# Two graph layers on one core: transposing the norms with VectorE and DRAM in place of TensorE

## Chip, core and metric

The kernel runs on one core of a Trainium2 chip. The metric is the device time of one execution in microseconds (us). The kernel before takes 2699.25 us, the median of three runs (2699.2 to 2702.12).

Names in the profile: PE is TensorE (its matrix products), PEld its weight loads, DVE is VectorE, ACT is ScalarE, POOL is GpSimd, SP is SyncE, which issues the transfers. All data is float32.

## What is computed

There are 64 graphs of 256 nodes with 512 features each (x is 64 x 256 x 512), and one adjacency matrix of 256 x 256 for all. Two layers follow each other, each with a norm ahead of it and x added after it. Cut to what matters:

```python
# layer 0
h = relu(layernorm(x))
hw = h @ W                                   # 512 -> 256
e = leaky_relu(hw @ a[0] + (hw @ a[1]).T, 0.2) + NEG * (1 - adj)
x = x + concat(softmax(e) @ hw, hw)
# layer 1: attention with 8 heads of 64
h = relu(layernorm(x))
q, k, v = (split_heads(h @ W.T + b) for W, b in ((Wq, bq), (Wk, bk), (Wv, bv)))
s = where(adj == 0, -inf, q @ k.T / 8)
x = x + (softmax(s) @ v) @ Wo.T + bo
```

## The kernel before

The graphs are taken two at a time: 32 groups of GB = 2 graphs (batches b), each batch of NT = 2 tiles of 128 nodes, so a group has GT = 4 tiles of 128 x 512. Of three groups in flight, one is in its attention, the next in its projections, the third in the first layer. Products with TensorE contract over the partitions, so the normed x (nodes on the partitions) has to be turned until the features lie on the partitions. This is done four times 128 x 128 for each tile:

```python
def norm_T(src, mv, name):
    ...                                          # ve = variance + EPS, on VectorE
    nc.gpsimd.tensor_tensor(rstd, ve, rexp, op=ALU.pow)     # 1 / sqrt, on GpSimd
    def normed(t):                               # on VectorE
        xn[t] = (src[t] - mean) * rstd           # (shortened; line 354)
    def put(t, dst):
        if t + 1 < GT:
            normed(t + 1)
        pt = mm(...)                             # a bank of PSUM
        for c in range(HP):                      # HP = 4
            transpose(pt[:, c, :], xn[t][:, c * P : (c + 1) * P], ident)   # TensorE
        nc.scalar.activation(dst, pt, AF.Relu)   # line 365
```

The projections and the last product are not made as eight block products but as seven, by the scheme of Strassen and Winograd. That scheme needs four sums of the operand's quadrants. GpSimd makes them, for the normed x (`sums`, 4 x 128x512 a group) and for the weighed values (`o_sums`, 4 x 128x256 a batch):

```python
def operand_sums(quads, sums):                   # lines 376 to 379
    a11, a12, a21, a22 = quads
    nc.gpsimd.tensor_add(sums[:, 0], a21, a22)
    nc.gpsimd.tensor_sub(sums[:, 1], sums[:, 0], a11)
    nc.gpsimd.tensor_sub(sums[:, 2], a11, a21)
    nc.gpsimd.tensor_sub(sums[:, 3], a12, sums[:, 1])
```

Attention goes by quads of four heads. `scores` makes sc on TensorE, exp on ScalarE, the product with the mask on VectorE and a first sum on GpSimd; `weigh`, one step later, makes the weighed values and their denominators:

```python
def scores(g, b, quad):
    for i in range(QH // 2):                     # two pairs of heads
        ...                                      # sc: two banks of PSUM
        for j in range(2):
            nc.scalar.activation(pair[:, j], sc[j], AF.Exp, scale=scale)         # line 572
        nc.vector.tensor_mul(pair, pair, maskT...)                               # line 573
        nc.gpsimd.tensor_add(ps[...], pair[:, :, 0, :], pair[:, :, 1, :])        # line 574

def weigh(g, b, quad, p, ps):
    ...                                          # pr: v times p; total: ones times ps
    nc.vector.reciprocal(r, total)               # line 604
    nc.vector.tensor_mul(oT[:, 2 * quad : 2 * quad + 2, :], pr, r...)            # line 605
```

`outputs` makes the last product py in seven parts, and VectorE adds each to x in place. The parts 1, 6, 5 and 3 accumulate in one bank of PSUM (`first`), the parts 2, 7 and 4 in another bank (7 and 4 share one). So each part has to wait until VectorE has read the one before it in the same bank:

```python
def outputs(g, b):
    sums = ...; operand_sums(halves(oT, P), sums)
    product(first, 1, True);   add(0, 0, first);  yield    # add: x += bank, line 628
    product(second, 2, True);  add(0, 0, second); yield
    product(first, 6, False);  add(1, 0, first);  yield
    product(second, 7, True);  add(1, 1, second); yield    # another bank
    product(first, 5, False);  add(1, 1, first);  yield
    product(second, 4, False); add(1, 0, second); yield
    product(first, 3, False);  add(0, 1, first)
    ...                                                    # out <- x
```

The main loop weaves these by strings. A group has four steps, one for each quad of each batch. u is one part of a projection (7 each of q, k and v), o one part of the last product, s one piece of the first layer (with the second norm at its end):

```python
steps = ("uosuoosuosoosuos", "uusususususu", "uosoosuosoosuos", "uusususususu")
for g in range(NG):
    projected = project(g + 1)
    short = first_layer(g + 2)
    for step, parts in enumerate(steps):
        weigh(*waiting)                          # of the step before
        if waiting[2] == NQ - 1: late = outputs(*waiting[:2])
        waiting = (g, b, quad, *scores(g, b, quad))
        if step == 1: load(g + 3)
        ...                                      # the string
```

Beside this the kernel judges whether its inputs allow exp without subtracting a maximum: `judge` bounds norms of the weights (products gram and square on TensorE). Its pieces lie in free places of the first groups. If it says no, a second version of the whole computation runs; for these inputs it does not. Most engines' order is left to a scheduler; only TensorE's is pinned to the order in the text.

Of the kernel before, what the change touches and what calls it, by code (L numbers as in the profile page):

```python
# [23 lines left out]
LARGEST_VALUE = 1e6  # L24

# [17 lines left out]
def bounded(  # L43
# [23 lines left out]
    nc = tc.nc  # L67
    B, N, D = x.shape
# [17 lines left out]
    psum = ctx.enter_context(tc.tile_pool(name="psum", bufs=1, space=bass.MemoryType.PSUM))  # L86

# [15 lines left out]


# [13 lines left out]
    xg = x.rearrange("(g b) (t p) d -> g p (b t) d", b=GB, p=P)  # L118
    og = out.rearrange("(g b) (t p) d -> g p (b t) d", b=GB, p=P)
# [3 lines left out]
    def load(g):  # L123
        xs[g] = big.tile([P, GT, D], F32, tag="x", name=f"x{g}", bufs=4)
        nc.sync.dma_start(xs[g], xg[g])

    load(0)


# [14 lines left out]
    for c in range(HP):  # L144
        for s in range(2):
            nc.vector.scalar_tensor_tensor(
                prod, w0_sb[:, c, 2:], 1.0, a_b[:, s, :], op0=ALU.mult, op1=ALU.mult,
                accum_out=w0_sb[:, c, s : s + 1],
            )
    edge = att.tile([P, NT, N], F32, tag="e", name="edge")  # L150
    nc.vector.tensor_scalar(edge, adj_i, 0.0, None, op0=ALU.not_equal)
# [6 lines left out]
    nc.vector.tensor_copy(maskT, pt)  # L158

    nc.vector.reduce_max(bad[:, 0, :], edge, axis=AX.X)  # L160
    nc.vector.tensor_scalar(bad[:, 0, :], bad[:, 0, :], 0.0, None, op0=ALU.is_equal)
    nc.vector.tensor_tensor(edge, edge, adj_i, op=ALU.not_equal)
    nc.vector.reduce_max(bad[:, 1, :], edge, axis=AX.X)

    load(1)
    load(2)


# [27 lines left out]
    rexp = const.tile([P, GT], F32, name="rexp")  # L196
    nc.gpsimd.memset(rexp, -0.5)
    ones = const.tile([P, P], F32, name="ones")
    nc.gpsimd.memset(ones, 1.0)

    def weight_sums(name):
        w = w_sb[name]
        first = nc.vector.tensor_sub(w[:, :, T3, :], w[:, :, W22, :], w[:, :, W12, :])
        after(first, latest[0])
        nc.vector.tensor_sub(w[:, :, T1, :], w[:, :, W12, :], w[:, :, W11, :])
        nc.vector.tensor_sub(w[:, :, T2, :], w[:, :, W22, :], w[:, :, T1, :])
        nc.vector.tensor_sub(w[:, :, T4, :], w[:, :, W21, :], w[:, :, T2, :])

    def last_bias():


        pb = mm("pb")
        for q in range(NQ):
            for half in range(2):
                b = small.tile([P, P], F32, tag="power", name=f"bv_{q}_{half}", bufs=1)
                nc.vector.tensor_scalar(b, ones, bv_col[:, half, q : q + 1], None, op0=ALU.mult)
                matmul(
                    pb, b, w_sb["o"][:, half, 2 * q : 2 * q + 2, :],
                    start=(q == 0 and half == 0), stop=(q == NQ - 1 and half == 1),
                )  # L220
        nc.vector.tensor_add(b_out, pb, b_out)


    def judge():
# [5 lines left out]
        nc.vector.memset(part, 0.0)  # L230
        junk = att.tile([P, D], F32, tag="junk", name="junk", bufs=1)

        def squares(col, *srcs):
            sums = small.tile([P, HP], F32, tag="sums", name=f"sums{col}", bufs=2)
            for i, src in enumerate(srcs):
                nc.scalar.activation(
                    junk[:, : src.free_size()], src, AF.Square, accum_out=sums[:, i : i + 1]
                )
            nc.vector.reduce_sum(part[:, col : col + 1], sums[:, : len(srcs)], axis=AX.X)

        for s in range(2):
            squares(s, w0_sb[:, :, s])
        squares(2, *[w0_sb[:, c, 2:] for c in range(HP)])
        wv = att.tile([P, HP, D // HP], F32, tag="block", name="wv_block", bufs=1)
        sums = small.tile([P, HP], F32, tag="sums", name="sums3", bufs=2)
        for c in range(HP):
            nc.sync.dma_start(
                wv, wvT[:, c * P : (c + 1) * P].rearrange("(c p) o -> p c o", p=P)
            )
            nc.scalar.activation(  # L250
                junk, wv.rearrange("p c o -> p (c o)"), AF.Square, accum_out=sums[:, c : c + 1]
            )
        nc.vector.reduce_sum(part[:, 3:4], sums, axis=AX.X)
        squares(4, bcol["q"])
        squares(5, bcol["k"])
        squares(6, bv_col.rearrange("p h q -> p (h q)"))
        nc.vector.reduce_max(part[:, 7:8], bad.rearrange("p a t -> p (a t)"), axis=AX.X)
        yield
        heads = const.tile([P, P], F32, name="heads")
        nc.vector.memset(heads, 0.0)  # L260
        for j in range(2):
            nc.vector.memset(heads[j * DH : (j + 1) * DH, j * DH : (j + 1) * DH], 1.0)
        rowsq = const.tile([P, 2, HP], F32, name="rowsq")
        for n, (name, src) in enumerate((("q", wqT), ("k", wkT))):
            for hp in range(HP):
                w = att.tile([P, HP, P], F32, tag="block", name=f"w{name}_block{hp}", bufs=1)
                nc.sync.dma_start(
                    w, src[:, hp * P : (hp + 1) * P].rearrange("(c p) o -> p c o", p=P)
                )
                yield  # L270
                gram = mm(f"gram_{name}{hp}")[:, :P]
                for c in range(HP):
                    matmul(
                        gram, w[:, c, :], w[:, c, :], start=(c == 0), stop=(c == HP - 1)
# [799 lines left out]
```

## Time and profile before

| what | value |
|---|---|
| time, median of 3 | 2699.25 us |
| span of the profiled run | 2697.3 us |
| granted TensorE clock | 0.993 |
| TensorE busy | 2620.4 us, 97% |
| VectorE busy | 1669.7 us, 62% |
| GpSimd busy | 1230.0 us, 46% |
| ScalarE busy | 835.9 us, 31% |
| moved by transfers | 78.49 MB, mean 29 GB/s |
| pt, the transposes of the norms | 1024 of 128x128 on TensorE |
| o_sums on GpSimd | 256 of 128x256, 727 to 1660 ns each in the mean of their line |
| mask multiply p on VectorE | 256 of 128x1024, mean 1588 ns |

A group of the profile is a line of the kernel with an engine, its operation, its result and operands, their shapes, the count, the busy time and the mean length of one. Idle time ahead of it is put down to the work whose end released it. In the timeline the first number is the start in us from the start of the span, the second the length of the merged instructions. Durations of TensorE overlap, as its instructions are pipelined; what one costs is therefore read from start to start.

### The profile page before, as it was taken

How to read it: one execution, taken by the hardware profiler on the slowest of the kernel's cores; microseconds unless marked ns; L12 is line 12 of the kernel's file. 1: busy time of each engine (PE TensorE's matmuls, PEld its weight loads, DVE VectorE, ACT ScalarE, POOL GpSimd, SP SyncE). 2: the span in 40 equal slices, each digit the busy share in tenths (PEclk: the TensorE clock that was granted, in tenths of full speed). 3: DMA queues.
4: the chain of work that ended last, by engine and by line, in shares of the span. 5: the costliest groups of instructions: out<-in, count | busy, mean ns of one | idle time of the engine just before them, and what ended most of it. 6: DMA issues, size and time to landing. Idle time of an engine off the chain costs nothing.

```text
span 2697.3 us, 41512 instructions
## 1 busy us (share of the span) xinstructions
PE 2620.4 (97%) x17150; PEld 2118.8 (79%) x17150; DVE 1669.7 (62%) x2558; ACT 835.9 (31%) x1771; POOL 1230.0 (46%) x1004
## 2 busy tenths in 40 slices
PE   5999999999999999999999999999999999999997
PEld 3888888878888887887788888788878878878874
DVE  5666566666557665566665576665576656666544
ACT  2333232333332333323333323333333333233321
POOL 2353355443445443545434454435455335445343
PEclk8999999999999999999999999999999999999998
DMA  5000101000001010000000000000000000000000
GB/s 164 1 12 32 36 24 36 13 32 32 28 32 36 9 36 32 24 32 9 32 32 24 32 32 9 32 32 24 32 32 9 32 32 24 32 17 23 17 16 25
DMA packets 45890, 78.49 MB, mean 29 GB/s; under 512 B 3712, under 2 KB 10624, under 8 KB 45696
## 3 DMA queue, kind: packets, MB, share of 16 engines
q1 hardware_dynamic: 45696, 75.77, 8.1%
q8 instruction: 137, 2.24, 0.3%
q14 instruction: 57, 0.47, 0.1%
HBM read 42.21 MB, written 33.55 MB: 28 GB/s over the span
## 4 chain that ended last, share of the span: by engine, by line
PE 89%; DVE 8%; POOL 1%; issue 1%; DMA 0%; ACT 0%; DVEq 0%
PE pq L113 15%; PE pv L113 14%; PE py L113 13%; PE pk L113 13%; PE pr L113 9%; PE ph L113 8%; PE sc L113 7%; PE po L113 4%; PE pt L116 4%; DVE p L573 3%; DVE r L604 2%; PE total L113 2%; DVE k L544 1%; DVE oT L605 1%; PE pn L116 1%
## 5 line engine op out<-in xcount | busy, mean ns | idle before, releaser
L573 DVE TENSOR_TENSOR p<-p,maskT 128x1024 f32<-128x1024 f32 x256 | 398.6, 1588 | 0.6 <-ACT p L572 0.5
L572 ACT ACTIVATE p<-sc 128x512 f32<-128x512 f32 x512 | 264.4, 602 | 380.9 <-PE sc L113 380.9
L574 POOL TENSOR_TENSOR ps<-p 128x512 f32<-128x512 f32 x256 | 366.2, 1447 | 0.0
L628 DVE TENSOR_TENSOR x<-py,x 128x256 f32<-128x256 f32 x448 | 187.6, 419 | 272.8 <-PE py L113 266.9
L604 DVE RECIPROCAL r<-total 128x256 f32<-128x256 f32 x128 | 224.5, 1754 | 194.6 <-PE total L113 194.6
L113 PE MATMUL py<-wo_sb,o_sums 128*128 128x256 f32 x1024 | 266.5, 384 | 26.4 <-DVE x L628 21.6
L420 POOL TENSOR_TENSOR x<-H,x 128x256 f32<-128x256 f32 x128 | 87.7, 685 | 443.0 <-ACT H L419 441.9
L113 PE MATMUL pr<-p,v 128*32 128x256 f32 x4096 | 251.8, 385 | 5.8 <-DVE p L573 5.8
L113 PE MATMUL sc<-q,k 64*128 64x256 f32 x2048 | 255.7, 389 | 0.0
L113 PE MATMUL pq<-sums,wq_sb 128*128 128x256 f32 x1024 | 246.7, 384 | 4.2 <-POOL sums L377 3.7
L113 PE MATMUL ph<-w_sb,hT 128*128 128x258 f32 x1024 | 246.1, 383 | 0.0
L113 PE MATMUL pk<-sums,wk_sb 128*128 128x256 f32 x1024 | 244.8, 382 | 0.0
L113 PE MATMUL pv<-wv_sb,sums 128*128 128x256 f32 x1024 | 242.0, 379 | 0.1
L113 PEld LDWEIGHTS sc<-q,k 64*128 64x128 f32 x2048 | 187.2, 186 | 69.7 <-issue 52.6
L113 PEld LDWEIGHTS py<-wo_sb,o_sums 128*128 128x128 f32 x1024 | 191.2, 192 | 62.9 <-POOL o_sums L377 37.6
L365 ACT ACTIVATE hT<-pt 128x512 f32<-128x512 f32 x256 | 153.1, 599 | 266.0 <-PE pt L116 265.7
L354 DVE TENSOR_SCALAR xn<-x,mv,rstd 128x512 f32<-128x512 f32 x256 | 225.8, 893 | 9.5 <-PE pt L116 4.9
L376 POOL TENSOR_TENSOR o_sums<-oT 128x256 f32<-128x256 f32 x64 | 106.2, 1660 | 262.6 <-DVE oT L605 262.6
L113 PEld LDWEIGHTS pq<-sums,wq_sb 128*128 128x128 f32 x1024 | 190.1, 191 | 39.1 <-issue 9.9
L113 PEld LDWEIGHTS ph<-w_sb,hT 128*128 128x128 f32 x1024 | 195.7, 192 | 28.6
L113 PEld LDWEIGHTS pk<-sums,wk_sb 128*128 128x128 f32 x1024 | 189.3, 190 | 33.9 <-issue 9.9
L113 PEld LDWEIGHTS pr<-p,v 128*32 128x32 f32 x4096 | 121.1, 110 | 112.2 <-issue 39.7
(145 smaller groups left out, 4054.4 us busy)
## 6 DMA issues: line engine op xcount, KB each, us to landing
x<-in_x_dram SPq DMA_DIRECT2D x32, 1024.0 KB, 5.5
out_dram<-x SPq DMA_DIRECT2D x64, 512.0 KB, 2.8
wq_sb<-in_L_gnn_Wq_dram SPq DMA_DIRECT2D x2, 512.0 KB, 11.7
wk_sb<-in_L_gnn_Wk_dram SPq DMA_DIRECT2D x2, 512.0 KB, 12.4
wv_sb<-in_L_gnn_Wv_dram SPq DMA_DIRECT2D x2, 512.0 KB, 11.4
wo_sb<-in_L_gnn_Wo_dram SPq DMA_DIRECT2D x8, 128.0 KB, 3.3
wv_block<-in_L_gnn_Wv_dram SPq DMA_DIRECT2D x4, 256.0 KB, 3.0
wq_block<-in_L_gnn_Wq_dram SPq DMA_DIRECT2D x4, 256.0 KB, 2.9
```

The source lines that it names most:

```text
L113: in_order(nc.tensor.matmul(*args, **kwargs))
L116: in_order(nc.tensor.transpose(*args))
L354: latest[0] = nc.vector.tensor_scalar(xn[t], src[:, t, :], mv[:, t, 0:1], rstd[:, t : t + 1], op0=ALU.subtract, op1=ALU.mult,).ins.name
L365: nc.scalar.activation(dst, pt, AF.Relu)
L376: nc.gpsimd.tensor_add(sums[:, 0], a21, a22)
L420: nc.gpsimd.tensor_add(xt[:, t, F1:], H[:, t, 2 : F1 + 2], xt[:, t, F1:])
L544: nc.vector.tensor_add(part(1, 1), first, p7)
L572: nc.scalar.activation(pair[:, j], sc[j], AF.Exp, scale=scale)
L573: nc.vector.tensor_mul(pair, pair, maskT[:, None, :, :].to_broadcast([P, 2, NT, N]))
L574: nc.gpsimd.tensor_add(ps[:, 2 * i : 2 * i + 2, :], pair[:, :, 0, :], pair[:, :, 1, :])
L604: nc.vector.reciprocal(r, total)
L628: nc.vector.tensor_add(to, out, to)
```

## The change

The norms' tiles are no longer turned by TensorE. VectorE turns each block of 32 by 32 in place (one instruction for a tile of 128 x 512), a transfer writes a batch's two tiles to DRAM (512 KB), and four transfers bring them back with the blocks at their places, 1 KB at a time. ScalarE then applies the relu from SBUF in place of PSUM. Group 0 still uses TensorE, as it has nothing to hide the transfers behind. The aim is to take the transposes off TensorE.

Further, VectorE makes the quadrant sums of the weighed values in place of GpSimd, right after the weighed values in its order. `not_sooner` pins an instruction behind the one of its engine that stands ahead of it in the text. The norm is made for each batch and not for each tile. The judge moves ahead of the main loop and takes its weights from what is loaded already. x is loaded by batch (7 buffers), and the bias of the last product is added to x one group later. The strings of the steps are as before, but the pieces of the first layer are cut anew, and some of them are empty to give the transfers time.

The diff, cut to its core:

```diff
+    def not_sooner(engine, operation, *args, **kwargs):
+
+        last = engine.last
+        after(getattr(engine, operation)(*args, **kwargs), last)
...
     def stats(mv, src, t, name):
...
+        if vector.last:
+            not_sooner(vector, "bn_stats", st, src[t])
...
+        def norm(b):
...
+            gpsimd.tensor_tensor(rstd, ve, rexp, op=ALU.pow)
+            for t in range(NT):
+                r = b * NT + t
+                xn[r] = att.tile([P, D], F32, tag="xn", name=f"xn{name}_{r}", bufs=2)
+                not_sooner(
+                    vector, "tensor_scalar", xn[r], src[r], mv[:, r, 0:1], rstd[:, t : t + 1],
+                    op0=ALU.subtract, op1=ALU.mult,
+                )
...
+            for t in tiles:
+                not_sooner(
+                    vector, "transpose",
+                    xt[:, :, :, t % NT, :], xn[t].rearrange("p (c j a) -> p j c a", j=J, a=S),
+                )
+                turned[t] = moved[:, :, :, t % NT, :].rearrange("p i c n -> p c i n")
+            nc.sync.dma_start(passed, xt.rearrange("p j c t n -> p j (c t n)"))
+            for j in range(J):
+                nc.sync.dma_start(
+                    moved[j * S : (j + 1) * S].rearrange("a i c t n -> a i (c t n)"),
+                    passed.rearrange("(i a) j e -> j a i e", a=S)[j],
+                )
...
+                    not_sooner(scalar, "activation", to, turned[b * NT + t], AF.Relu)
...
+    def operand_sums(engine, quads, sums):
         a11, a12, a21, a22 = quads
-        nc.gpsimd.tensor_add(sums[:, 0], a21, a22)
...
+        not_sooner(engine, "tensor_add", sums[:, 0], a21, a22)
+        engine.tensor_sub(sums[:, 1], sums[:, 0], a11)
...
     def first_layer(g):
...
+        norm(0)
         yield GAP
...
+        turn(0)
+        norm(1)
+        yield GAP
+        turn(1)
+        yield GAP
+        yield GAP
+        put(0, hT[0])
+        yield GAP
+        for r in range(GT):
...
+            if r == NT - 1:
+                put(1, hT[1])
...
+            if r == 2:
+                norm(0)
+            elif r == 3:
+                turn(0)
...
+        norm(1)
         yield GAP
...
+        turn(1)
+        yield GAP
+        put(0, hT[:, :, :N])
+        yield GAP
+        put(1, hT[:, :, N:])
...
+        operand_sums(gpsimd, quads, sums)
...
     def weigh(g, b, quad, p, ps):
...
         if quad == NQ - 1:
             places.append(v_tag)
...
+            operand_sums(vector, quads, sums)
...
+            if step == 1 and g + 1 < NG:
+                residual(g + 1)
+            if step % 2 and g + 3 < NG:
+                load(g + 3, b)
```

## The prediction

> **What bounds the kernel now.** I read the table of busy shares first, then the slices, then the waits of TensorE, and last the timeline of one group in the middle of the run. From the page:
>
> ```profile
> PE 2620.4 (97%) x17150; PEld 2118.8 (79%) x17150; DVE 1669.7 (62%) x2558; ACT 835.9 (31%) x1771; POOL 1230.0 (46%) x1004
> PE   5999999999999999999999999999999999999997
> ```
>
> TensorE works in every slice but the first and the last at 9 tenths or more; its waits by releaser sum to few microseconds (the largest, py on x of L628, is 21.6 us of 2697). So a microsecond of matrix work taken away is a microsecond won, unless another engine then makes TensorE wait. What the transposes cost is read from the timeline of TensorE by start times, since the durations there overlap:
>
> ```profile
> 1001.68 0.60 PE L116 MATMUL pt<-ident,xn 128*128 128x128 f32 x4
> 1002.11 1.89 PE L113 MATMUL pv<-wv_sb,sums 128*128 128x256 f32 x8
> 1003.84 0.60 PE L116 MATMUL pt<-ident,xn 128*128 128x128 f32 x4
> ```
>
> A burst of four transposes (one 128x512 tile) takes 1002.11 - 1001.68 = 0.43 us, one product of the projections 1.73 us. There are 8 bursts a group (2 norms, 4 tiles), 256 in the run.
>
> 62% for VectorE is a mean. One group is four steps (a step is weigh, scores, and what its string of u, o and s adds). I cut the group at the starts of pr and asked for the busy time by engine in the four stretches:
>
> ```profile
> 1010.43:1031.09 20.66, 20.66 (x140) 17.00 (x139) 10.79 (x15) 6.75 (x14) 12.10 (x10) 1.00 0.00 1
> 1031.09:1053.70 22.61, 22.61 (x145) 18.53 (x144) 7.68 (x9) 8.01 (x19) 7.10 (x6) 1.00 0.20 71
> 1053.70:1073.90 20.20, 19.58 (x127) 15.64 (x126) 16.00 (x30) 5.03 (x11) 6.41 (x5) 1.00 0.00 1
> 1073.90:1092.39 18.49, 18.49 (x132) 15.01 (x131) 16.93 (x27) 6.39 (x13) 12.69 (x10) 1.00 0.08 30
> ```
>
> The columns are length, then PE, weight loads, DVE, ACT, POOL busy. TensorE fills all four; VectorE is busy 16.0 of 20.2 us in step 2 and 16.9 of 18.5 in step 3, but only 10.8 and 7.7 in steps 0 and 1.
>
> [...] no transpose is in this trace, but bn_stats over the same 512 elements is 691 ns (median), so I take 0.65 us from start to start for one tile: an estimate from that row. [...] the mask multiply (L573) takes 1212 ns at least, 1742 at the median, 2291 at most. [...]
>
> ```profile
> 1012.87 1.76 DVE L604 RECIPROCAL r<-total 128x256 f32<-128x256 f32 x1 [3.35 <-PE total L113]
> 1014.66 0.69 DVE L605 TENSOR_TENSOR oT<-pr,r 128x512 f32<-128x512 f32 x1
> 1015.26 3.23 DVE L573 TENSOR_TENSOR p<-p,maskT 128x1024 f32<-128x1024 f32 x2
> 1018.42 0.41 DVE L628 TENSOR_TENSOR x<-py,x 128x256 f32<-128x256 f32 x1
> ```
>
> Two multiplies take 3.23 us in place of 2.4, beside GpSimd's o_sums. The reader is also to see the chain: from the reciprocal at 1012.87 to the first x at 1018.42, all in VectorE's own order. The third product py, at 1020.16, writes the bank that this x has to have read first.
>
> **Part 1, removed from TensorE.** Groups 1 to 31 lose 8 bursts each: 248 x 0.43 = 107 us. TensorE's work by step then is: step 0, 20.66 less 3 bursts (1.30), one ph that moves to step 1 (1.75) and a square of the judge (0.22) = 17.4; step 1, 22.61 + 1.75 - 0.43 = 23.9; step 2, 20.20 less a wait (0.62) and a square (0.22) = 19.4; step 3, 18.49 - 4 x 0.43 - 0.22 = 16.5. Sum 77.2 in place of 81.96: without any new wait -4.7 us a group, over some 30 groups -140 us, 2560 us.
>
> **Part 2, added to VectorE.** 248 transposes x 0.65 = 161 us, and 64 x 4 sums of 128x256 at some 0.35 us from start to start (x of L628, same size, is 0.42 long) = 90 us. 1670 + 251 = 1921 us still is below 2560. But where it stands counts. In the built program's order of VectorE, all of the first norm now lies in step 0, pinned behind what precedes it: 4 bn_stats, 4 xn, 4 transposes, and 3 of the o_sums. In the kernel before, the bn_stats of that norm run in the last step of the group ahead. That makes 10.79 + 2.7 (bn_stats) + 0.7 (aggr) + 1.1 (two more xn) + 2.6 (transposes) + 1.1 (o_sums) - 0.3 = 18.7 us of VectorE in a step with 17.4 us of TensorE, and it can't begin before the step's reciprocal at +2.44.
>
> **Step 0 followed through** (us from the start of pr). VectorE: r 2.44, oT 4.23, first p 4.83 to 6.05, three o_sums to 7.1, second p to 8.3, x of py1 to 8.7; then bn, bn, q, bn, x, bn to 12.5. GpSimd: ps (1.25, behind the first p) 6.1 to 7.35, four sums (4 x 1.24) to 12.3, second ps to 13.6, power for rstd (1.02) to 14.6. Now two xn to 15.7 and only then x of the third py: 16.1. TensorE would be ready for the fifth py at about 13.5, but that writes the same bank and waits to 16.1 (about 2.6). Then two transposes stand ahead of x of the next py (about 1.0 more of waiting), a second power, two xn and two transposes ahead of the one after it (1.0 more). Step 0 becomes about 22.3 us even if VectorE and GpSimd never block each other. With strict alternation (three o_sums and the second p against ps and the sums, each up to one 1.25 us instruction later) the second p ends at 12, the third py waits 3 us, and I come to about 25. With no wait for GpSimd at all, VectorE alone from 2.44 gives 20.4.
>
> **Step 2**: three o_sums ahead of x of the first py put it at 9.7 to 10.7, where before it ended at 8.7; the third py waits 1.8 to 2.7. 21.1 to 22 us. Steps 1 and 3 have slack: 23.9 and 16.5.
>
> **Part 3, the transfers.** 4 x (512 KB out, 512 KB back) a group is 4.2 MB in some 85 us, about 49 GB/s beside the 29 of now: no bound. One path is issue 0.4 + 2.8 (a store of 512 KB lands in 2.8 us on the page) + 4 issues (1.5) + about 3 = 8 us. The second batch of the second norm is tightest: turned at about 12 of step 3, landed at about +4 of the next step, where ScalarE takes it between two exponentials. GpSimd's sums so start some 8 us later than now (now 1010.65, with the step). That is in the count above.
>
> **Part 4, the judge.** It moves ahead of the groups. Its some 12 us of TensorE leave the steps (counted above, 0.66 us in this group) and join a start in which TensorE had gaps; the last outputs lose the slow o_sums of GpSimd (1.6 us each). I take both as nought together.
>
> **Sum.** 22.3 to 25 + 23.9 + 21.1 to 22 + 16.5 = 83.8 to 87.4 us a group against 81.96: +1.8 to +5.4, middle +3.6. Times 30: +108. 2699 + 108 = about 2805 us.
>
> **Rivals.**
> 1. VectorE has room everywhere and the waits don't come: 2560 us (-5%). For it: 62% busy, 107 us of TensorE work gone, and order pins that look thought out. Against it: the order in step 0, where x of py stands behind work that waits for GpSimd.
> 2. VectorE alone bounds step 0, with no waiting for the power and no blocking: 20.4 + 23.9 + 20.5 + 16.5 = 81.3, so 2680: the gain is just given back. For it: GpSimd loses o_sums (350 us of its 1230).
> 3. The transfers hold up ScalarE, which holds up the scores: to over 2900. For it: the store and the reads of both batches share one queue, and the reads of the first stand behind the store of the second. Against it: the 8 us fit.
>
> **Range and chances.** The two counts of step 0 give 2753 to 2861; rival 2 sets the floor, rival 3 the top: 2700 to 2880. Faster by over 2% needs under 79.9 us a group, which only rival 1 gives: 0.13. Within 2%: 0.19. Slower: 0.68.
>
> **What would show it.** After the change: pt in TensorE only for group 0; TensorE's largest wait is py on VectorE's x, hundreds of microseconds with that of pq on sums; step 0 is 22 to 25 us, step 3 about 16.5; VectorE waits for rstd of GpSimd about once or twice a group; a transpose is about 0.65 to 0.7 us. I am wrong if step 0 is under 20 us, or if TensorE waits for ScalarE behind transfers.

## The result, and the profile after

The changed kernel takes 2925.61 us (median of 4 runs, 2922.37 to 2926.53), the kernel before 2700.49 us on the same chip (4 runs): a ratio of 1.0831, with a 95% interval of 1.0812 to 1.085. The prediction was 2805 us, range 2700 to 2880. The direction and most of the mechanism were right; the loss is 225 us and not 106.

A few more names stand in the lines below. pq, pk and pv are the parts of the projections, q, k and v VectorE's additions to them, and kept_v a part that ScalarE copies because it is needed once more. ph and po are products of the first layer. xt holds the blocks that VectorE has turned, passed and moved the same in DRAM and back in SBUF, and hT the normed x, turned and rectified. r is the reciprocal of the denominators, and oT the weighed values.

In the kernel after, most instructions of VectorE, ScalarE and GpSimd carry line L35 (the helper that remembers the last instruction), and all products L135; they are told apart by their tiles. The busy shares and TensorE's slices, from the page of the kernel after:

```profile
PE 2610.7 (89%) x16158; PEld 2053.3 (70%) x16158; DVE 1977.3 (68%) x3103; ACT 820.5 (28%) x1759; POOL 932.6 (32%) x816
...
PE   6799998899898899898999988998988998989997
```

TensorE has 992 instructions fewer, as meant, but it no longer fills its slices. What it waits for (us in total, times, longest), from the waits of TensorE after:

```profile
PE py L135 <- DVE x L35: 212.2, 134, 3.4
PE pv L135 <- ACT kept_v L35: 40.7, 30, 1.6
...
PE pq L135 <- POOL sums L35: 10.2, 2, 7.6
```

The same four steps of one group, cut at the starts of pr (length, then PE, weight loads, DVE, ACT, POOL busy, TensorE's granted clock, share and GB/s of the transfers):

```profile
1004.85:1027.99 23.14, 18.44 (x117) 13.63 (x116) 19.29 (x32) 6.08 (x13) 10.30 (x8) 1.00 0.08 34
1027.99:1051.91 23.92, 23.92 (x149) 19.67 (x148) 8.90 (x10) 9.36 (x22) 5.34 (x6) 1.00 0.37 100
1051.91:1075.29 23.38, 21.07 (x125) 16.59 (x125) 18.19 (x35) 5.03 (x11) 5.69 (x5) 0.93 0.00 1
1075.29:1093.40 18.11, 16.77 (x113) 13.13 (x112) 14.90 (x19) 4.87 (x9) 7.61 (x7) 1.00 0.53 175
```

The sum is 88.55 us against 81.96. Over the run: the first pr starts at 142.6 us (127.0 before), thirty groups take 2656.9 us (2456.0), and from the start of the last full group to the end it is 124.1 us (114.3). So the span's +226.3 us are +15.6 at the start, +200.9 (6.7 a group) in the middle, +9.8 at the end.

**Step 0.** VectorE and TensorE in the first step of that group:

```profile
1009.68 1.22 DVE L35 TENSOR_TENSOR p<-p,maskT 128x1024 f32<-128x1024 f32 x1
1010.82 0.42 DVE L35 TENSOR_TENSOR o_sums<-oT 128x256 f32<-128x256 f32 x1
1011.27 1.37 DVE L35 TENSOR_TENSOR o_sums<-o_sums,oT 128x256 f32<-128x256 f32 x1
1012.68 1.37 DVE L35 TENSOR_TENSOR o_sums<-oT,o_sums 128x256 f32<-128x256 f32 x1
1013.97 2.28 DVE L35 TENSOR_TENSOR p<-p,maskT 128x1024 f32<-128x1024 f32 x1
1016.17 0.41 DVE L35 TENSOR_TENSOR x<-py,x 128x256 f32<-128x256 f32 x1
```

```profile
1013.49 1.03 PE L135 MATMUL py<-wo_sb,oT 128*128 128x256 f32 x4
1016.64 1.13 PE L135 MATMUL py<-wo_sb,o_sums 128*128 128x256 f32 x4 [2.12 <-DVE x L35]
...
1022.33 1.13 PE L135 MATMUL py<-wo_sb,o_sums 128*128 128x256 f32 x4 [1.97 <-DVE x L35]
1023.91 1.13 PE L135 MATMUL py<-wo_sb,oT 128*128 128x256 f32 x4 [0.45 <-DVE x L35]
```

GpSimd's sums of the normed x run from 1012.3 to 1018.7 here, late because hT has come through DRAM. While GpSimd runs its first sum ps (from 1011.0) and then these sums, two of VectorE's o_sums take 1.37 us in place of 0.42, and the second mask product 2.28 in place of 1.22. The addition x at 1016.17 stands behind all of them, and the third product py waits 2.12 us for it. The next waits are for x behind the norms and transposes.

**Step 2.** The third py waits 2.31 us, and then TensorE's granted clock is 0.50 for 3.4 us. TensorE's timeline, and the windows of 1 us behind the wait (the last three columns are the granted clock, where 0.50 is half speed, and the transfers' share and GB/s):

```profile
1062.16 1.13 PE L135 MATMUL py<-wo_sb,o_sums 128*128 128x256 f32 x4 [2.31 <-DVE x L35]
1063.13 1.87 PE L135 MATMUL po<-H,e 128*128 128x257 f32 x4
1064.79 2.79 PE L135 MATMUL pk<-hT,wk_sb 128*128 128x256 f32 x8
```

```profile
1063.00:1064.00 1.00, 1.00 (x5) 0.79 (x4) 0.42 (x1) 0.00 (x0) 0.00 (x0) 0.59 0.00 0
1064.00:1065.00 1.00, 1.00 (x4) 0.81 (x3) 0.00 (x0) 0.00 (x0) 0.00 (x0) 0.50 0.00 0
1065.00:1066.00 1.00, 1.00 (x3) 0.81 (x3) 0.83 (x3) 0.00 (x0) 0.00 (x0) 0.50 0.00 0
1066.00:1067.00 1.00, 1.00 (x5) 0.79 (x4) 0.70 (x2) 0.00 (x0) 0.00 (x0) 0.70 0.00 0
```

Eight products pk take 2.79 us, and 1.89 elsewhere. In the thirty groups from the first pr on, 29 such halved stretches of 3.4 us begin in step 2, and 8 in step 0. The clock lost over the run can be read from the page: (1 - mean clock) x span is (1 - 0.971) x 2923.6 = 85 us, before (1 - 0.993) x 2697.3 = 19 us. So up to 66 us of the 226 are clock and not waiting. The figure (1 - mean clock) x span is called the clock loss below.

**Step 3.** ScalarE's third copy of a product that is kept comes late, and pv waits for it (ScalarE, then TensorE):

```profile
1089.12 0.59 ACT L35 COPY kept_v<-pv 128x512 f32<-128x512 f32 x1 [3.53 <-DVE v L35]
```

```profile
1089.75 1.99 PE L135 MATMUL pv<-wv_sb,hT 128*128 128x256 f32 x8 [1.34 <-ACT kept_v L35]
```

The copy waits 3.53 us for VectorE's addition v, which frees a buffer. The diff has a line that the prediction passed over: three buffers for the kept products became two.

```diff
-                s = att.tile([P, 2, N], F32, tag=f"kept{i}", name=f"kept{i}_{name}_{g}", bufs=1)
+                s = att.tile([P, 2, N], F32, tag="kept", name=f"kept{i}_{name}_{g}")   # the pool's 2
```

### The profile page after: what moved, and what is told of

It is laid out like the page before. It is cut to its first block, busy times and chain, and to the rows that moved or that the text cites. A ratio compares the mean times of both kernels' runs of the same rounds, so it can differ in the third digit from the quotient of the medians.

```text
span 2923.6 us, 40862 instructions
## 1 busy us (share of the span) xinstructions
PE 2610.7 (89%) x16158; PEld 2053.3 (70%) x16158; DVE 1977.3 (68%) x3103; ACT 820.5 (28%) x1759; POOL 932.6 (32%) x816
## 4 chain that ended last, share of the span: by engine, by line
PE 49%; DVE 42%; ACT 4%; issue 3%; POOL 1%; DMA 1%; SPq 0%; ACTq 0%; DVEq 0%; POOLq 0%
PE pk L135 10%; DVE p L35 9%; PE py L135 8%; PE ph L135 8%; DVE o_sums L35 7%; PE pq L135 7%; DVE r L35 6%; PE po L135 5%; PE pr L135 4%; PE pv L135 4%; DVE xt L35 4%; DVE st L35 3%; DVE xn L35 3%; DVE x L35 2%; PE sc L135 2%
## 5 line engine op out<-in xcount | busy, mean ns | idle before, releaser
L35 POOL TENSOR_TENSOR ps<-p 128x512 f32<-128x512 f32 x256 | 350.2, 1368 | 1120.7 <-DVE p L35 1108.8
L135 PE MATMUL py<-wo_sb,o_sums 128*128 128x256 f32 x1024 | 287.0, 406 | 202.6 <-DVE x L35 202.6
L35 DVE TENSOR_TENSOR p<-p,maskT 128x1024 f32<-128x1024 f32 x256 | 410.7, 1605 | 4.2 <-ACT p L35 4.1
L35 ACT ACTIVATE p<-sc 128x512 f32<-128x512 f32 x512 | 267.4, 602 | 413.5 <-PE sc L135 413.5
L135 PEld LDWEIGHTS py<-wo_sb,o_sums 128*128 128x128 f32 x1024 | 190.4, 195 | 270.3 <-DVE x L35 248.0
L35 DVE RECIPROCAL r<-total 128x256 f32<-128x256 f32 x128 | 223.8, 1749 | 189.7 <-PE total L135 189.7
L35 DVE TENSOR_TENSOR k<-pk,kept_k 128x512 f32<-128x512 f32 x96 | 65.9, 687 | 291.8 <-PE pk L135 291.6
L135 PE MATMUL pq<-sums,wq_sb 128*128 128x256 f32 x1024 | 249.2, 387 | 11.5 <-POOL sums L35 10.2
L135 PE MATMUL pr<-p,v 128*32 128x256 f32 x4096 | 252.2, 385 | 7.4 <-DVE p L35 7.4
L35 POOL TENSOR_TENSOR rstd<-ve,rexp 128x2 f32<-128x2 f32 x128 | 90.8, 710 | 524.8 <-DVE ve L35 503.8
L135 PE MATMUL sc<-q,k 64*128 64x256 f32 x2048 | 256.3, 390 | 0.0
L135 PE MATMUL ph<-w_sb,hT 128*128 128x258 f32 x1024 | 244.6, 382 | 1.9 <-ACT hT L35 1.9
L135 PE MATMUL pk<-sums,wk_sb 128*128 128x256 f32 x1024 | 244.9, 382 | 0.0
L35 DVE TENSOR_TENSOR x<-py,x 128x256 f32<-128x256 f32 x448 | 181.7, 410 | 84.1 <-PE py L135 80.5
L135 PEld LDWEIGHTS sc<-q,k 64*128 64x128 f32 x2048 | 187.7, 187 | 70.2 <-issue 53.0
L135 PE MATMUL pv<-wv_sb,sums 128*128 128x256 f32 x1024 | 231.6, 379 | 1.7 <-DVE v L35 1.7
L135 PEld LDWEIGHTS pq<-sums,wq_sb 128*128 128x128 f32 x1024 | 194.8, 193 | 49.8 <-POOL sums L35 10.8
L135 PE MATMUL pv<-wv_sb,hT 128*128 128x256 f32 x768 | 182.7, 387 | 40.7 <-ACT kept_v L35 40.7
L135 PEld LDWEIGHTS ph<-w_sb,hT 128*128 128x128 f32 x1024 | 195.2, 191 | 30.9 <-ACT hT L35 2.7
L135 PEld LDWEIGHTS pv<-wv_sb,sums 128*128 128x128 f32 x1024 | 194.5, 190 | 28.5 <-DVE v L35 2.1
L135 PEld LDWEIGHTS pk<-sums,wk_sb 128*128 128x128 f32 x1024 | 189.3, 190 | 33.8 <-issue 9.9
L135 PE MATMUL py<-wo_sb,oT 128*128 128x256 f32 x768 | 202.2, 395 | 11.4 <-DVE x L35 9.6
```

What stands on the lines that cost most here:

```text
L35: instruction = getattr(self.engine, operation)(*args, **kwargs)
L135: in_order(nc.tensor.matmul(*args, **kwargs))
```

## The experiments

The theory: TensorE's saving is real, and the loss is made of waits in three steps. VectorE's own order (o_sums, mask product, norms and transposes ahead of an output addition) causes those of steps 0 and 2; GpSimd's late sums stretch it, and the clock adds to it. The rivals: the work as such is too much for VectorE, or one of the two parts that were moved, the sums or the transposes, explains all alone. A time given without an interval is of one run; the kernel before took 2699.29 us beside the first four, 2702.3 beside the next four. Step lengths are from starts of pr, of one group in the middle of the run; clock loss as above. In four rows the groups differ by where a halved stretch falls, and the group shown is not the usual one, or not the only one: step 0 of first_layer_by_vector is 21.3 us in 17 of 28 groups in the middle of the run, step 2 of three_kept 21.7 in 19 of 28, step 3 of norm_unpinned 24.5 to 24.8 in 19 of 28, and step 0 of no_transit 21.9 or 22.2 in 8 of 28.

| kernel | time, us | step 0 | step 1 | step 2 | step 3 | clock loss, us |
|---|---|---|---|---|---|---|
| before | 2700.49 | 20.66 | 22.61 | 20.20 | 18.49 | 19 |
| after | 2925.61 | 23.14 | 23.92 | 23.38 | 18.11 | 85 |
| step2_product_between | 2840.36 | 23.14 | 23.92 | 19.96 | 18.61 | 60 |
| osums_b0_gpsimd | 2822.81 | 23.38 | 23.93 | 20.20 | 18.12 | 42 |
| turned_by_tensor | 2815.83 | 20.40 | 24.80 | 21.69 | 18.25 | 25 |
| norm_unpinned | 3055.37 | 21.55 | 23.92 | 23.38 | 23.96 | 150 |
| both_undone | 2734.09 | 19.67 | 24.80 | 20.21 | 18.26 | 11 |
| no_transit | 2819.98 | 20.67 | 23.92 | 21.70 | 18.12 | 51 |
| second_mask_behind_x | 2829.54 | 22.80 | 23.93 | 20.69 | 18.11 | 59 |
| three_kept | 2886.90 | 23.88 | 25.33 | 23.24 | 16.51 | 89 |
| first_layer_by_vector | 2712.64 | 19.59 | 23.93 | 19.11 | 18.26 | 49 |
| none_by_vector | 2688.55 | 19.33 | 24.80 | 19.12 | 18.26 | 11 |
| second_layer_by_vector | 2745.97 | 22.53 | 24.80 | 19.11 | 16.51 | 41 |
| first_layer_spread | 2686.53 | 19.19 | 23.93 | 19.11 | 18.26 | 19 |

**step2_product_between.** Another part of a projection between the second and third py of step 2 gives VectorE time.

```diff
-    steps = ("uosuoosuosoosuos", "uusususususu", "uosoosuosoosuos", "uusususususu")
+    steps = ("uosuoosuosoosuos", "uusususususu", "uoosuosoosuosos", "uusususususu")
```

> One string changed: in step 2 the second part of the k projection in that step (1.73 us of TensorE) stands ahead of the third py in place of behind the first po. The work is the same. Theory (VectorE's x of the first py comes late behind the o_sums, TensorE idles 2.3 us, and the idle time makes the chip halve TensorE's clock for the next 3.4 us): the wait falls from 2.3 to about 0.6 us and the slow stretch (1.7 us lost) vanishes, step 2 goes from 23.4 to about 20 us, the granted clock from 0.971 to about 0.99, the time by about 29 x 3.4 = 100 us to about 2825 us. Rival (the low clock comes from something else, such as power or the transfers): only the wait goes, about 29 x 1.7 = 50 us, to 2875 us, and the clock stays at 0.97.

Step 2 falls from 23.38 to 19.96 us, and its wait from 2.31 to 0.58. No halved stretch is left in it, so the clock follows the wait, and the rival falls for this step. The time comes near the theory's number, but the whole gains 85 us and not the 100 that 30 x 3.4 would be, and the clock 0.979 and not 0.99. Step 3 grows by 0.5 us, as pv's wait for the kept product goes from 1.36 to 1.84, and 24 halved stretches now follow waits of step 0, where there were 8 (60 us of clock loss are left). So mending step 2 also moved the halved stretches of step 0.

**osums_b0_gpsimd.** Only the first batch's sums of the weighed values go back to GpSimd.

```diff
-            operand_sums(vector, quads, sums)
+            operand_sums(gpsimd if b == 0 else vector, quads, sums)
```

> The sums of the weighed values go back to GpSimd for the first graph of each group only (the one whose last product lies in step 2); the second graph's stay on VectorE. Theory (the three o_sums ahead of x of the first py are what makes the third py wait in step 2): the wait falls from 2.3 us to about 0.6 as before the change, the slow clock goes, step 2 about 20 us, the time about 2825 us; step 0 stays at about 23 us. Rival (VectorE is simply full, whatever the order): VectorE loses about 1.5 us of work a group, so about 2880 us.

The time is 2822.81 us, as the theory had it. Step 2 is as before the change (20.20), with 0.85 us of waiting. The four sums of one batch on VectorE, three of them (2.2 us) in step 2 ahead of x, cost the run 103 us; 43 of these are clock loss.

**turned_by_tensor.** All norms are turned by TensorE again, without DRAM; the sums stay on VectorE.

```diff
-        by_pe = g == 0
+        by_pe = True
+            # put(b): mm bank, 4 transposes by ident for each tile, then ScalarE's relu
```

> All norms turned by TensorE again, just ahead of the relu, as before the change; everything else of the change stays (o_sums on VectorE, norm by graph and pinned, two kept buffers, the judge ahead). No transfer through DRAM. My theory is that the transposes on VectorE are not the main loss: TensorE gets back 8 x 0.43 = 3.4 us a group, against which the waits behind the transposes go (about 1.0 us in step 0, 1 to 1.5 us in step 3), so 2925 + 30 x (1 to 1.5) = about 2960 us. Rival (transposes on VectorE or their way through DRAM are what costs): the time falls to about 2700 to 2760 us.

Theory and rival both missed: the time is 2815.83 us. The 107 us of transposes are back on TensorE, and yet the kernel is 110 us faster. Step 0's third py now waits only 0.33 us although the o_sums still stand ahead of it, because GpSimd's sums come at the start of the step, ahead of VectorE's. So the way through DRAM was stretching one of the o_sums and the second mask product; I had put these waits down to the o_sums alone. But 60 of the 110 us are clock loss (85 to 25), and most of that is luck: the third py of step 2 still waits 2.31 us, as in the kernel after. There a halved stretch followed in each of the 28 groups in the middle of the run; here it followed in 3. Nor does it hang on who turns the norms: in no_transit, where VectorE turns them as in the kernel after, it followed the same wait in 8 of 28 groups.

**norm_unpinned.** The pins of VectorE are left out, and the scheduler places the norm.

```diff
+        if engine is not vector:
             after(instruction, last)
```

> The pins of VectorE's instructions are left out (those of ScalarE and GpSimd stay); the scheduler then puts the first norm with its transposes into step 3 of the group ahead, in place of step 0. Theory (the place of this work ahead of the x of py makes TensorE wait in step 0): the waits at the fifth, fourth and third-last py of step 0 go (3.2 us a group), but step 3 now holds 23 us of VectorE in 18 us and delays the start of step 0's chain by some 2 us, so 30 x 1 to 3 us less: 2830 to 2890 us. Rival (only the amount of VectorE's work counts): 2925 us, no change.

The time, 3055.37 us, misses the theory and its rival. The scheduler put statistics, norms and transposes of the first layer into step 3, ahead of VectorE's v additions; step 3 grows to some 24 us, and the third py of step 0 waits 3.2 us. From the waits of TensorE:

```profile
PE pv L137 <- DVE v L35: 122.3, 30, 4.2
```

The work is the same as after the change, and the run is 130 us longer, 65 of them clock loss. So with the same amount of work, its place alone moves the time by 130 us. For this kernel the pins are better than the scheduler's order.

**both_undone.** Transposes on TensorE and all o_sums on GpSimd; the rest of the change stays.

```diff
-        by_pe = g == 0
+        by_pe = True
-            operand_sums(vector, quads, sums)
+            operand_sums(gpsimd, quads, sums)
```

> Both named parts of the change undone (norms transposed by TensorE, the quadrant sums of the weighed values on GpSimd); everything else of the change kept (loads by batch element, the new order of the norms, two buffers for the kept products, the rewritten judge). Theory (the two parts are the cause, and their costs of about 105 and 110 us add up): 2695 to 2730 us, no wait of over 0.6 us for py6. Rival (something else in the change costs too, such as the two kept buffers at 1.5 us a group): 2740 to 2780 us.

The time is 2734.09 us, 4 above the band, and waits of py that the theory excluded are there: 1.16 us in step 0 and 0.85 in step 2. Undone alone, the sums of one batch had given 103 us and the transposes 110; both, with the other batch's sums besides, give 191. Clock losses of 43, 60 and 74 us are in these three figures, so they don't say how far the two costs overlap. The rest of the change costs 32 us, as a group takes 82.94 us in place of 81.96. No wait for a kept product appears here or in turned_by_tensor: the two buffers hurt only beside the transposes.

**no_transit.** The transfers are left out, and ScalarE reads the blocks unmoved. The output therefore isn't the reference's; VectorE's and TensorE's work is that of the kernel after.

```diff
-            nc.sync.dma_start(passed, xt.rearrange("p j c t n -> p j (c t n)"))
-            for j in range(J):
-                nc.sync.dma_start(moved[...], passed[...])
-                turned[t] = moved[:, :, :, t % NT, :]...
+                turned[t] = xt[:, :, :, t % NT, :]...
```

> The transfers to DRAM and back are left out: ScalarE's rectifier reads the blocks as VectorE turned them, so the output is not the reference's; VectorE's work is the same. Theory (the latency of the transfers, some 6 to 8 us, shifts GpSimd's operand sums onto VectorE's second mask product and o_sums, and makes py6 wait 2.1 us in step 0 and in step 2): the waits fall or move, 2840 to 2890 us. Rival (VectorE's own 1.3 us a batch element and the order of its queue are what costs): 2910 to 2935 us, as with the transfers.

The time is 2819.98 us: 106 us less, which is more than the theory's band has. GpSimd and VectorE in step 0, which begins at 1051.60 here:

```profile
1051.82 2.52 POOL L35 TENSOR_TENSOR sums<-hT 128x512 f32<-128x512 f32 x2 [5.48 <-PE pv L135]
```

```profile
1059.66 1.21 DVE L35 TENSOR_TENSOR p<-p,maskT 128x1024 f32<-128x1024 f32 x1
1060.80 0.41 DVE L35 TENSOR_TENSOR o_sums<-oT,o_sums 128x256 f32<-128x256 f32 x1
1061.13 0.41 DVE L35 TENSOR_TENSOR x<-py,x 128x256 f32<-128x256 f32 x1
```

The sums begin with the step and not 7.5 us into it, the second mask product takes 1.21 us and not 2.28, and x stands 9.5 us after the step's start in place of 11.3. The waits fall from 2.12 and 1.97 to 0.33 and 1.29 us. So what the transfers cost in step 0 is that GpSimd's sums move onto VectorE's work. Beside that, the first pr starts 16 us earlier, and 34 of the 106 us are clock loss (51 in place of 85): in step 2, with the same 2.31 us of waiting, the halved stretch stays away in 20 of 28 groups (21.70 us in place of 23.38).

**second_mask_behind_x.** The second mask product stands behind the first output addition.

```diff
+                else:
+                    not_sooner(vector, "tensor_mul", pair, pair, maskT...)   # called after "uo", not in scores
```

> Every product and sum is computed; in the steps with an output projection VectorE's second multiplication by the mask is pinned behind the first output addition, so that it no longer stands between o_sums and that addition. Theory (the wait of py6 in steps 0 and 2 is o_sums plus the second mask product [...], and step 2 loses another 1.7 us to the halved clock after it): both waits fall by 1.2 to 2.3 us, the halved clock goes, 2780 to 2850 us. Rival (the mask product only moves the wait to the next products or to the weighed values of the next step): 2910 us or more.

The time, 2829.54 us, is within the theory's band, but the case is not clean: step 2's wait falls to 1.30 us, while in step 0 the sums, pushed back in turn, make pq wait 1.87 us. From the waits of TensorE in this kernel:

```profile
PE py L135 <- DVE x L35: 83.5, 90, 2.1
PE pq L135 <- POOL sums L35: 64.8, 32, 6.9
```

Over the run, py's waits for x fall by 129 us (from 212.2) and pq's for the sums grow by 55 (from 10.2). So a good part of the wait moved, as the rival said, and the larger part went. Of the 96 us gained, 26 are clock loss; the halved stretches of step 2 are gone, and 22 stand in step 0.

**three_kept.** Three buffers for the kept products again; the room comes from one buffer in place of two for the blocks that VectorE has turned.

```diff
-            xt = att.tile([...], F32, tag="xt", name=f"xt{name}_{b}")
+            xt = att.tile([...], F32, tag="xt", name=f"xt{name}_{b}", bufs=1)
-                s = att.tile([P, 2, N], F32, tag="kept", name=f"kept{i}_{name}_{g}")
+                s = att.tile([P, 2, N], F32, tag="kept", name=f"kept{i}_{name}_{g}", bufs=3)
```

> Three buffers for the kept products as before the change (room made by one buffer in place of two for the transposed blocks). Theory (the third kept product waits for VectorE's late v addition only because the buffers went from three to two; 1.3 to 1.6 us a group): the wait of pv on ScalarE's kept product goes, 2870 to 2895 us. Rival (VectorE is late with the next v addition anyway, so the wait moves on to pv on VectorE's addition): 2910 to 2930 us.

The time, 2886.90 us, is in the band. The window of step 3 in this kernel:

```profile
1059.65:1076.16 16.51, 16.51 (x113) 13.21 (x113) 14.82 (x19) 4.87 (x9) 7.62 (x7) 1.00 0.53 174
```

TensorE fills it, and it has the predicted 16.5 us. The buffers cost 1.6 us a group. The total is no clean measure of that, and that it lies in the band is partly luck. Step 1 grows by 1.41 us, as ph waits 1.15 us for hT; I put this down to the single buffer for the blocks, which is not shown. And the halved stretches fall elsewhere: in step 2, with the same wait of 2.31 us, in 9 of 28 groups in place of all, and in step 0 31 times in place of 8.

**first_layer_by_vector, none_by_vector, second_layer_by_vector.** Three versions with the same order of VectorE's queue: the second mask product behind x, and the statistics of a group's second batch one piece later. The first two have all o_sums on GpSimd, the third only the first batch's. The third also has the buffers of three_kept.

```diff
-        norm, turn, put = norm_T(xt, mv, f"0_{g}", by_pe)        # first layer
+        norm, turn, put = norm_T(xt, mv, f"0_{g}", g == 0)       # by VectorE; True: by TensorE
-        norm, turn, put = norm_T(xt, mv, f"1_{g}", by_pe)        # second layer
+        norm, turn, put = norm_T(xt, mv, f"1_{g}", True)         # by TensorE; g == 0: by VectorE
-        for t in range(GT):
+        for t in range(NT):                                      # the others: ahead of norm(1)
             stats(mv, xt, t, f"0_{g}")
```

> Everything is computed. The first layer's norms go by VectorE and DRAM (two batch elements a group, 1.7 us of TensorE saved), the second layer's by TensorE again, so that the operand sums come early; both batch elements' quadrant sums back on GpSimd; the second mask product behind the first output addition; the statistics of the second batch element emitted one piece later. Theory (the loss is one of placement: VectorE's queue ahead of an output addition, sums that come late and meet VectorE): per group about 18.3 (step 3) + 18.5 (step 0) + 23.9 (step 1) + 20.0 (step 2) = 80.7 us, against 81.96 before: 2640 to 2690 us, granted clock at least 0.99. Rival (any transposing on VectorE costs what it saves): 2700 to 2740 us.

The time is 2712.64 us against 2699.97 before, a ratio of 1.0043 (1.0026 to 1.006), which is the number of the rival. Step 2 is 19.1 us without any wait, but in step 0 the sixth py waits 1.95 us: the wait has moved there from the third and the fifth. VectorE and TensorE there:

```profile
1119.15 1.30 DVE L35 STREAM_TRANSPOSE xt<-xn 128x512 f32<-128x512 f32 x2
1120.37 0.65 DVE L35 BATCH_NORM_STATS2 st<-x 128x6 f32<-128x512 f32 x1
1120.94 0.40 DVE L35 TENSOR_TENSOR x<-py,x 128x256 f32<-128x256 f32 x1
```

```profile
1121.40 1.13 PE L135 MATMUL py<-wo_sb,oT 128*128 128x256 f32 x4 [1.95 <-DVE x L35]
```

An addition of 0.40 us stands behind two transposes and a bn_stats. In 17 of 28 groups a halved stretch follows (step 0 is 21.3 us then, and the group 82.6). In 10 it does not, and the group takes 80.9 us, where the theory had 80.7. So the theory's sum of steps came true in these, its clock of 0.99 (it is 0.982) and its total did not.

> As the version beside it, but both layers' norms are transposed by TensorE: only the order of VectorE's queue differs from the run with both parts undone. Theory: the waits of py6 (1.16 us in step 0, 0.85 us in step 2) go, 82.9 - 2.0 = 81 us a group, 2665 to 2700 us; above the version beside it by what the first layer's transposes save, up to 50 us. Rival (the waits move elsewhere): 2720 to 2740 us.

The time is 2688.55 us, a ratio of 0.9958 (0.9941 to 0.9975), within the theory's band: order alone, with no transpose on VectorE, brings 45 us against both_undone, and the kernel is 0.4% faster than the kernel before. A wait of 0.82 us of the sixth py in step 0 is left. But the theory also had this version up to 50 us above first_layer_by_vector, and it is 24 us below: the 0.6 us a group that the transposes save there at full clock (80.9 against 81.5) is more than lost to halved stretches (clock loss 49 us against 11).

> The mirror image: the second layer's norms by VectorE and DRAM, the first layer's by TensorE; three kept buffers; the sums of the weighed values on GpSimd for the first batch element and on VectorE for the second; the order of the queue as in the two versions beside it. Theory (the second layer's transfers are what delays GpSimd's operand sums into step 0, so this half of the change is the costly one): step 3 16.5, step 0 19 to 21, step 1 24.8, step 2 20.0, 80.3 to 82.3 us a group, 2660 to 2730 us, above the version with the first layer by VectorE. Rival (it makes no difference which layer): within 10 us of it.

The time is 2745.97 us, a ratio of 1.0167 (1.015 to 1.0184): 16 us above the band, and 33 us above its mirror image. The theory had it above too, but the two differ in more than the layer (the second batch's o_sums and the buffers), so that the layer alone makes the difference is not shown. Step 3 is 16.51 us, so the transposes and three buffers save what they should there. Step 0 gives it back: pq waits 1.87 us for sums that come 7.5 us into the step, and then the sixth py waits 1.7 us or a halved stretch follows.

**first_layer_spread.** As first_layer_by_vector, with the first layer's norm and transposes of a batch one piece later each.

```diff
-        norm(0)
         yield GAP
-        turn(0)
+        norm(0)
         for t in range(NT, GT):
             stats(mv, xt, t, f"0_{g}")
+        yield GAP
+        turn(0)
         norm(1)
         yield GAP
         turn(1)
         yield GAP
-        yield GAP
         put(0, hT[0])
```

> As first_layer_by_vector (first layer's norms by VectorE and DRAM, second layer's by TensorE, quadrant sums on GpSimd, second mask product behind the first output addition), with the norm of the first batch element and its transposes emitted one piece later each, so that an output addition of 0.4 us no longer stands behind two statistics, two norms and two transposes. Theory (1.93 us of wait for py6 in step 0 and the half clock after it are a matter of VectorE's order alone): step 0 from 19.6-21.3 us to 17.5-18.5 us, 79.0 to 80.5 us a group, 2630 to 2670 us, clock 0.99 or more. Rival (the wait moves to ph of step 1, which then waits for the later transfer, or to the next output product): 2690 to 2720 us.

The time is 2686.53 us against 2699.54, a ratio of 0.9948 (0.9931 to 0.9964): 0.5% faster than the kernel before, and 26 us faster than the version it mends, but short of the band. A group takes 80.5 us, the clock loss is back at 19 us, and the sixth py's wait in step 0 is 1.55 us, so step 0 is 19.2 us where the theory had 17.5 to 18.5. The rival was partly right: ph waits for hT 24.3 us in all, 7.0 of them in the first step, which begins at 137.2 us (130.1 in none_by_vector) and takes 33.4 us in place of 24.8. Start and later waits of ph are why it only draws level with none_by_vector, whose groups are 1 us longer.

## Why the prediction was right or wrong

Three steps of the prediction failed. The sum of step 2 ended at the wait and left out the halved clock behind it (1.8 us a group). Step 3 was said to have slack, and there TensorE waits for a buffer (1.6 us a group). Start and end were taken as nought together (25 us). The chain of waits in step 0, the heart of the prediction, came true.

**TensorE's work (part 1): right.** Where nothing waits, step 3 is 16.51 us (predicted 16.5; three_kept), step 1 23.92 (23.9), step 2 19.11 (19.4), and step 0 17.37 (17.4; at the end of first_layer_spread, where no first layer is left). So 77 us a group is what TensorE needs without waits, as predicted. (Its waits before did not sum to "few microseconds": they are 71 us by the same list, most of them at the two ends of the run.)

**VectorE's added work (part 2): the transposes right, the sums too small.** 248 transposes take 159.6 us (161 predicted). The 256 o_sums take 228.1 us in the kernel after, and not 90: 0.89 us each, as GpSimd's ps and sums run beside them. VectorE's total, 1977 against 1921 us, hides this, since the 256 norms xn became shorter at the same time (165.1 us in place of 225.8). no_transit and turned_by_tensor show what ran beside the o_sums in step 0: with GpSimd's sums early (in no_transit they end at 1056.91, and the first o_sum starts at 1057.92), the third o_sum there is back at 0.41 us and the second mask product at 1.21. The second o_sum keeps its 1.37 us, beside ps (1.38 us from 1058.07).

**Step 0: right.** 22.3 to 25 us were predicted (the 25 was an estimate, with VectorE and GpSimd strictly taking turns), 23.14 and 23.7 measured. The chain was the predicted one (the third py behind o_sums and the second mask product, the fifth behind norms), with waits shorter than the counts: 2.12 in place of 3, 1.97 in place of 2.6, and 0.45 and 0.16 in place of the two of 1.0.

**Step 2: the wait right, the sum wrong.** The third py was to wait 1.8 to 2.7 us; it waits 2.31. But I ended the account at the wait: "21.1 to 22 us". It is 23.38, because the clock is halved for 3.4 us after it; without the wait the halved stretch is gone too (step2_product_between). With the same wait and the full clock it is 21.70 (no_transit, turned_by_tensor), inside the predicted figure. So the missing term is 1.7 us, and it came in 29 of the thirty groups.

**Step 3: wrong.** "Steps 1 and 3 have slack" was read from TensorE's and VectorE's busy time, without asking when buffers come free. The kept products have two buffers in place of three, and VectorE is late in this step behind its norms and transposes: 18.11 us in place of 16.5. both_undone, with two buffers and no such wait, shows that it takes the transposes too; three_kept shows that a third buffer ends it.

**The transfers (part 3): right.** They land in 2.9 and 3.2 us (medians), and ScalarE waits for them only 4.6 us in the whole run. That the sums come some 8 us later was counted (7.5 measured).

**Start and end (part 4): wrong.** Taken as nought together, they are +15.6 and +9.8 us; 7.6 of the first are pq's wait for GpSimd's sums, which come through DRAM. In no_transit the first pr starts at 126.7 us, as before the change (127.0), so all of the +15.6 comes with the transfers, which have little to hide behind at the start. The +9.8 at the end was not taken apart.

**The sum.** The middle of the predicted groups is 85.6 us and the measured mean 88.56; 3.0 x 30 = 89 us, and start and end add 25. These are 114 of the 121 us between 2805 and 2925.61; the rest is rounding, and that a group of the kernel before takes 81.87 us in the mean and not 81.96. Of the 3.0 us, step 2 (23.38 against 21.55) is +1.8, step 3 +1.6 and step 0 -0.5.

**The rivals.** The first (no waits) and the second (VectorE alone bounds step 0, at 20.4 us) fall by the waits. The second returns once the sums come early: with the same work on VectorE, step 0 of no_transit is 20.67 us where no halved stretch falls in it. (The 20.40 of turned_by_tensor is no sign of it, as VectorE has no transposes there.) The third, transfers that hold up ScalarE, came nearest in its number and was wrong in its mechanism. The line for a gain of 2% was misplaced a little: 54 us over 30 groups is 80.2 us a group, not 79.9; nothing hangs on it.

## What to carry to other kernels

An engine at 62% can still hold the key: before moving work to it, write down its queue for each stage and look which short instruction, here an addition of 0.4 us that frees a bank, ends up behind the new work; mending that order was worth 45 us with no work moved at all. Where the granted clock falls after a wait of TensorE, count the wait at more than its length, and compare versions by their waits and their full-clock steps before their totals: a wait of 2.31 us cost 1.7 us more in 28 of 28 groups of one kernel and in 3 of 28 of another. Check every buffer count that a diff changes. A transfer that hides well (ScalarE waits 4.6 us for these in the whole run) may still shift what follows it onto another engine's busy stretch (here GpSimd's sums, by 7.5 us).

## What the runs showed of the hardware

**Where the clock is halved.** From the windows of 1 us, the halved stretches of the kernel after between 1060 and 1420 us begin at 1063.18 (a clock of 0.59 is 0.18 us at full and 0.82 at half speed), 1110.97, 1151.93, 1240.68, 1329.42, 1377.21 and 1418.16 us, each some 3.4 us long.

The length of the wait alone doesn't decide whether one follows. In the kernel after, a halved stretch followed the wait of 2.31 us in step 2 and one of 1.97 us in step 0 (to 1110.88). None followed the 1.97 us that ended at 1022.33, nor the 2.12 us that ended at 1016.64.

The wait of step 2 makes it a wider test, as five kernels have it at 2.30 to 2.54 us (after, turned_by_tensor, no_transit, three_kept, norm_unpinned), 140 times in the middle of their runs. A halved stretch followed in 68 of the 140. In the kernel after it was 28 of 28, in turned_by_tensor 3 of 28. Here, in turned_by_tensor, the clock stays full behind the same wait:

```profile
1108.22 1.13 PE L135 MATMUL py<-wo_sb,o_sums 128*128 128x256 f32 x4 [2.31 <-DVE x L35]
```

```profile
1109.00:1110.00 1.00, 1.00 (x6) 0.90 (x5) 0.42 (x1) 0.00 (x0) 0.00 (x0) 1.00 0.00 0
```

What decides between the two was not shown.
